# Starting a second wavefront earlier, and issuing a second layer in another order

## The chip, the cores and the metric

The kernel runs on one core of a Trainium2 chip. The time is that of the device for one execution, in microseconds (us). Before the change it is 12678.93 us, the median of three runs (12673.02 to 12680.4). A core has five engines, each with a queue of its own that it works off in order: TensorE (PE, with weight loads shown apart as PEld), VectorE (DVE), ScalarE (ACT), GpSimd (POOL), and SyncE (SP), which here only issues transfers (DMA). ACT issues some transfers too.

## The reference

The input is a batch of 16 images, 64 x 64 pixels, 128 channels, in float32. Two layers follow each other, each as x + layer(groupnorm(x)) with 32 groups of four channels.

The first layer is a two-dimensional recurrence. The cell at row i, column j needs h and c of the cell above and of the cell to the left:

```
f0 = sigmoid(pf0 + h_u @ uf0);  f1 = sigmoid(pf1 + h_l @ uf1);  hsum = h_u + h_l
it = sigmoid(pi + hsum @ ui);   ot = sigmoid(po + hsum @ uo);   cp = tanh(pc + hsum @ uc)
c  = f0*c_u + f1*c_l + it*cp;   h  = ot * tanh(c)
```

The p's are products of the normed pixel with weights of 128 x 128.

The second layer is a Mamba block (256 inner channels, 16 states, a causal convolution of four taps) over the 4096 pixels of each image, once forwards and once backwards; the results are added:

```
h = dA_t * h + dBx_t;   y_t = sum over states of h * C_t      (for each channel and state)
y = (y + xc * D) * silu(z);   out = y @ out_w.T
```

## The kernel before

**First layer** (`layer0`, L761 to L941). Cells on one anti-diagonal of an image do not need each other. So the work goes diagonal by diagonal: 127 diagonals (`ND`), of 1 to 64 and back to 1 cells. The 16 images are two groups of eight; a group is a *wavefront* (w = 0 or 1), and a diagonal of n cells is one tile of 128 channels x 8n columns.

- `statistics(b, q)` (L781) loads a quarter of image b on SP's queue (512 KB into `xs`, a ring of four buffers), transposes it on PE in eight blocks, and takes two DVE statistics. Four such *sets* make an image. The 32 sets of wavefront 0 run first; `normal(0)` (L805) makes scale and shift of the group norm from them. The 32 sets of wavefront 1 are `rest`.
- `load` (L841) reads the pixels of a diagonal, transposes and norms them (L855, L860). `cell` (L863) forms five gates: for each, a product with the pixel (L877) and one with the state (L878), accumulated in one PSUM bank, then an activation (L881). Then come the products with the old cell state on POOL (L889) and DVE (L890), input gate times candidate (L891), two additions (L892, L893), tanh on ACT (L894), and h on DVE (L895). `store` (L897) transposes h back, adds it to the pixels and writes `x1` from ACT's queue (L912).
- The list `steps` (L916 to L918) sets the order. Wavefront 1 begins `LATER` = 32 + 2 = 34 diagonals behind wavefront 0. So wavefront 0 is alone for 34 diagonals, then 93 pairs (one diagonal of each) follow, then wavefront 1 is alone for 34.
- A step does one piece of side work (L924 to L933): a set of statistics while `rest` has any; then `normal(1)`; then the zeroing of one of 12 matrices in memory; then a piece of `begin`, the start of the second layer: its weights, reading image 0 in eight parts, its group norm and its eight normalisations. The weights come from step 81 on, the rest from three steps after wavefront 0 has finished.

Within the first layer a scheduler at build time orders the instructions of each queue from this program.

**Second layer** (`layer1`, L944 on). An image is 16 *passes*: eight pieces of 512 pixels forwards (passes 0 to 7), and eight backwards (8 to 15). A pass has, for each of two halves of the 256 channels, 16 scans over 512 pixels on DVE (L1305), one for each state; ACT makes the decays (L1251); POOL makes 12 products of states with C (`out_of`, L1328), four drives (L1259) and two smaller products (`times`, L1232); PE makes the other drives (`drive_rows`, L1285), the convolution (`conv`, L1122), the sums over the states in transposed form (`sums`, L1365), and several transposes and projections. A backward pass has more for PE: the gate (L1141), adding the stored forward result (`again`), and the projection back (L1420, L1440). In forward passes the next image is read (L1038 to L1056); its group norm (`normal`, L1060 with L732 to L744) comes in pass 1, followed by eight normalisations on ACT (L1068). SP's queue issues all transfers of the layer, among them the states carried between passes (`keep`, L1317), the spread rows (L1204, L1210) and the scattered matrices (L1268, L1275).

The order of issue of all engines comes from `order_of_issue` (L300): it lists every operation of all 16 images with an engine, a cost (`COST`), what it must follow, and which ring of buffers it takes from (`RINGS`). `simulate` (L573) then runs through planned time; whenever an engine is free it takes, of the operations that are ready, the one with the least due time. The due time is 16 for each pass begun plus the operation's entry in the table `URGENCY` (L89). It has a number for every kind of operation in a pass, apart for forward and backward passes. The instructions are issued in exactly the order that comes out. So a change in the table moves operations within the queues, but neither adds nor drops any.

Of the kernel before, what the change touches and what calls it, by code (L numbers as in the profile page):

```python
# [8 lines left out]
F32 = mybir.dt.float32  # L9
# [5 lines left out]
P = 128  # L15
B, HH, WW, C = 16, 64, 64, 128
# [8 lines left out]
T = 512  # L25
# [19 lines left out]
def units_of(order):  # L45

    count = {}
    for x in order:
# [4 lines left out]
        else:  # L53
# [37 lines left out]
        {(0, 0): -19.08, (0, 1): 208.77, (0, 2): 213.67, (0, 3): 242.61, (1, 0): -194.98, (1, 1): -170.3,  # L91
         (1, 2): -208.38, (1, 3): -208.83},
        {(0, 0): 148.19, (0, 1): 250, (0, 2): 249.74, (0, 3): 231.08, (1, 0): -185.59, (1, 1): -186.03,
         (1, 2): -176.29, (1, 3): -177.49},
    ),
    "xproj": (
        {(): -6.34},
        {(): 83.3},
    ),
    "xproj_take": (  # L100
        {(): 46.52},
        {(): -25.9},
    ),
    "rows": (
        {(): 10.88},
        {(): -173.37},
    ),
    "bturn": (
        {(): 216.27},
        {(): -247.72},  # L110
    ),
    "bturn_take": (
        {(): -10.16},
        {(): 155.72},
    ),
    "dtproj": (
        {(0,): -166.35, (1,): -49.09},
        {(0,): -234.94, (1,): -199.34},
    ),
    "times": (  # L120
        {(0,): -141.19, (1,): -141.5},
        {(0,): -190.57, (1,): -223.42},
    ),
    "turn": (
        {(0,): 231.47, (1,): -199.74},
        {(0,): 155.15, (1,): 101.59},
    ),
    "turn_take": (
        {(0,): 35.4, (1,): 33.43},
        {(0,): 227.22, (1,): 227.05},  # L130
    ),
    "skip": (
        {(0,): -85.09, (1,): 194.24},
        {(0,): -59.43, (1,): 211.98},
    ),
    "spread": (
        {("b", 0): 55.31, ("d", 0): 221.01, ("c", 0): 249.78, ("c", 1): 249.59, ("d", 1): -104.59, ("c",
         2): 74.43, ("c", 3): 179.65, ("b", 1): 235.3, ("d", 2): 178.23, ("c", 4): 117.53, ("c", 5):
         216.75, ("k", 0): 205.82},
        {("b", 0): 49.04, ("d", 0): 82.05, ("c", 0): 58.5, ("c", 1): 225.69, ("d", 1): 85.64, ("c", 2):  # L140
         -52.53, ("c", 3): -84.56, ("b", 1): -71, ("d", 2): 188.69, ("c", 4): -46.09, ("c", 5): 139.95,
         ("k", 0): 79.7},
    ),
    "drive": (
        {(0, 0): -117.16, (1, 0): -45.65, (0, 1): -106.02, (1, 1): 204.54},
        {(0, 0): -55.01, (1, 0): -101.65, (0, 1): 78.56, (1, 1): 78.33},
    ),
    "decay": (
        {(0, 0): 214.71, (4, 0): 231.6, (5, 0): 235.97, (6, 0): 250, (7, 0): 244.04, (1, 0): -226.9, (8,
         0): 242.45, (9, 0): 229.56, (10, 0): 250, (11, 0): 196.68, (2, 0): 245.22, (12, 0): 142.99, (13,  # L150
         0): 196.62, (14, 0): 218.85, (15, 0): 250, (3, 0): 235.27, (4, 1): 237.55, (5, 1): 56.83, (6,
         1): 236.39, (7, 1): 200.04, (0, 1): 59.98, (8, 1): 241.45, (9, 1): 238.35, (10, 1): 238.37, (11,
         1): 237.94, (1, 1): 48.96, (12, 1): 223.29, (13, 1): 109.79, (14, 1): 109.58, (15, 1): 193.48,
         (2, 1): 244.06, (3, 1): 190.67},
        {(0, 0): 219.27, (4, 0): 159.93, (5, 0): 228.42, (6, 0): 227.96, (7, 0): 233.04, (1, 0): 162.12,
         (8, 0): 236.54, (9, 0): 145.98, (10, 0): -139.12, (11, 0): -88.73, (2, 0): -99.75, (12, 0):
         157.46, (13, 0): 250, (14, 0): 156.85, (15, 0): 167.22, (3, 0): 239.69, (4, 1): 187.28, (5, 1):
         236.16, (6, 1): 225.96, (7, 1): 248.99, (0, 1): 67.98, (8, 1): 248.77, (9, 1): 49.99, (10, 1):
         242.8, (11, 1): 168.72, (1, 1): 67.45, (12, 1): 163.7, (13, 1): 244.57, (14, 1): 244.31, (15,
         1): 176.22, (2, 1): 178.59, (3, 1): 181.09},  # L160
    ),
    "scan": (
        {(0, 0): -215.99, (4, 0): -197.78, (5, 0): -201.82, (6, 0): 171.7, (7, 0): -200.28, (1, 0):
         208.99, (8, 0): 81.27, (9, 0): 69.78, (10, 0): 50.84, (11, 0): 80.97, (2, 0): -179.33, (12, 0):
         -157.48, (13, 0): -159.07, (14, 0): -158.42, (15, 0): -158.71, (3, 0): -148.7, (4, 1): 17.61,
         (5, 1): 34.08, (6, 1): 7.6, (7, 1): 7.23, (0, 1): 145.62, (8, 1): 26.88, (9, 1): 56.47, (10, 1):
         26.63, (11, 1): 52.08, (1, 1): 203.51, (12, 1): 173.49, (13, 1): 174.73, (14, 1): 173.35, (15,
         1): 173.11, (2, 1): 173.02, (3, 1): -185.61},
        {(0, 0): 211.65, (4, 0): 208.82, (5, 0): 213.32, (6, 0): 210.34, (7, 0): 234.88, (1, 0): 234.81,
         (8, 0): 82.08, (9, 0): 81.92, (10, 0): 11.04, (11, 0): 61.9, (2, 0): 80.26, (12, 0): 96.06, (13,  # L170
         0): 93.07, (14, 0): 44.04, (15, 0): 82.19, (3, 0): 68.39, (4, 1): -115.05, (5, 1): -159.13, (6,
         1): -144.43, (7, 1): -169.42, (0, 1): -152.48, (8, 1): -158.76, (9, 1): -192.29, (10, 1):
         -192.53, (11, 1): -193.7, (1, 1): 178.94, (12, 1): 148.84, (13, 1): 136.94, (14, 1): 136.65,
         (15, 1): 184.35, (2, 1): 182.44, (3, 1): 227.69},
    ),
    "scatter": (
        {("d", 0): -98.3, ("d", 1): 226.02, ("d", 2): -35.02, ("k", 0): 142.02},
        {("d", 0): 197.57, ("d", 1): 181.75, ("d", 2): -137.41, ("k", 0): 53.02},
    ),
    "drive_rows": (  # L180
        {(0, 0): 86.02, (1, 0): -84.84, (2, 0): 123.21, (0, 1): 206.34, (1, 1): 117.75, (2, 1): 194.74},
        {(0, 0): 241.28, (1, 0): -59.19, (2, 0): -162.71, (0, 1): -157.55, (1, 1): -215.22, (2, 1):
         175.52},
    ),
    "keep": (
        {(0, 0): 250, (1, 0): -11.9, (2, 0): 227.54, (3, 0): -221.6, (4, 0): 195.72, (5, 0): -92.62, (0,
         1): 62.29, (1, 1): 169.33, (2, 1): 81.35, (3, 1): -229.04, (4, 1): 142.26, (5, 1): -18.73},
        {(0, 0): -186.63, (1, 0): 100.75, (2, 0): 123.12, (3, 0): -226.46, (4, 0): 126.26, (5, 0):
         182.78, (0, 1): -126.19, (1, 1): 179.51, (2, 1): -247.02, (3, 1): -146.55, (4, 1): -45.3, (5,
         1): 57.7},  # L190
    ),
    "out_of": (
        {(0, 0): 6.28, (1, 0): 110.81, (2, 0): 0.41, (3, 0): 46.99, (4, 0): 204.64, (5, 0): 230.6, (0,
         1): 26.46, (1, 1): 164.53, (2, 1): -138.94, (3, 1): -244.66, (4, 1): -239.51, (5, 1): -149.12},
        {(0, 0): -174.66, (1, 0): -174.81, (2, 0): 72.48, (3, 0): 7.85, (4, 0): 129.81, (5, 0): 102.68,
         (0, 1): -122.95, (1, 1): -122.04, (2, 1): -117.06, (3, 1): -192.11, (4, 1): -39.91, (5, 1): 57.1},
    ),
    "sums": (
        {(0, 0): 147.01, (1, 0): 204.95, (2, 0): 18.42, (3, 0): 110.12, (4, 0): -165.71, (5, 0): -154.21,
         (0, 1): 227.07, (1, 1): 180.09, (2, 1): 194.99, (3, 1): 242.48, (4, 1): 216.64, (5, 1): -169.16},  # L200
        {(0, 0): -212.32, (1, 0): -162.81, (2, 0): -161.63, (3, 0): -161.82, (4, 0): -157.85, (5, 0):
         -158.54, (0, 1): 73.85, (1, 1): 109.31, (2, 1): 81.83, (3, 1): 248.19, (4, 1): 249.43, (5, 1):
         249.81},
    ),
    "keep_group": (
        {(0, 0): -194.35, (0, 1): -163.44},
        {(0, 0): -239.33, (0, 1): -182.43},
    ),
    "turned": (
        {(0, 0, 0): -203.27, (0, 0, 1): 190.03, (0, 0, 2): 9.82, (0, 0, 3): -96.4, (0, 1, 0): 229.53, (0,  # L210
         1, 1): -154.5, (0, 1, 2): -157.58, (0, 1, 3): -113.93},
        {(0, 0, 0): -157.81, (0, 0, 1): 123.6, (0, 0, 2): -144.76, (0, 0, 3): -39.63, (0, 1, 0): 248.86,
         (0, 1, 1): 248.61, (0, 1, 2): 248.52, (0, 1, 3): 239.67},
    ),
    "turned_take": (
        {(0, 0, 0): 113.8, (0, 0, 1): 75.95, (0, 0, 2): 42.34, (0, 0, 3): 42.24, (0, 1, 0): 247.32, (0,
         1, 1): 153.61, (0, 1, 2): 153.43, (0, 1, 3): 222},
        {(0, 0, 0): 64.54, (0, 0, 1): 69.77, (0, 0, 2): 68.43, (0, 0, 3): 67.62, (0, 1, 0): -249.7, (0,
         1, 1): -214.46, (0, 1, 2): 155.94, (0, 1, 3): 155.85},
    ),  # L220
    "weigh": (
        {(0, 0): -250, (0, 1): -131.3},
        {(0, 0): -179.49, (0, 1): -150.84},
    ),
    "finish": (
        {(0,): 43.55, (1,): 250},
        {(0,): -158.64, (1,): 234.04},
    ),
    "spill": (
        {(): 111.19},  # L230
        {},
    ),
    "read_load": (
        {(): -159.46},
        {},
    ),
    "read_turn": (
        {(): 120.8},
        {},
    ),  # L240
    "read_take": (
        {(): 144.64},
        {},
    ),
    "read_stats": (
        {(): 1.05},
        {},
    ),
    "gate": (
        {},  # L250
        {(0,): -158.22, (1,): -164.04},
    ),
    "recall": (
        {},
        {(): -141.83},
    ),
    "again": (
# [1238 lines left out]
```

## Time and profile before

The profile is of one execution of its own, which took 12716.73 us.

| | |
|---|---|
| median of 3 runs | 12678.93 us |
| profiled execution | 12716.73 us, span 12714.9 us |
| granted TensorE clock, mean | 0.993 |
| PE busy / PE weight loads | 12144.3 us (96%) / 9452.5 us (74%) |
| DVE / ACT / POOL busy | 11120.1 (87%) / 9944.8 (78%) / 10600.8 us (83%) |
| first write of h / last write of h (end of first layer) | 89.1 / 1553.1 us |
| POOL products of states with C (L1328) | 3072, 2430 ns each |
| DVE scans with a drive from PE (L1305) | 5376, 1261 ns each, next one starting before the last ends |

How to read it: times are microseconds from the start of the span, and means of one instruction are in ns. An instruction's line is that of the kernel before. "out<-in" names the tile written and those read. A bracket `[1.2 <-PE py]` says that the engine was idle 1.2 us before the instruction, and which instruction ended that. PE overlaps its instructions and their ends are modelled; the distance from one start to the next is the safer measure. The granted clock is the share of full speed that PE was given.

### The profile page before, as it was taken

How to read it: one execution, taken by the hardware profiler on the slowest of the kernel's cores; microseconds unless marked ns; L12 is line 12 of the kernel's file. 1: busy time of each engine (PE TensorE's matmuls, PEld its weight loads, DVE VectorE, ACT ScalarE, POOL GpSimd, SP SyncE). 2: the span in 40 equal slices, each digit the busy share in tenths (PEclk: the TensorE clock that was granted, in tenths of full speed). 3: DMA queues.
4: the chain of work that ended last, by engine and by line, in shares of the span. 5: the costliest groups of instructions: out<-in, count | busy, mean ns of one | idle time of the engine just before them, and what ended most of it. 6: DMA issues, size and time to landing. Idle time of an engine off the chain costs nothing. (4 is left out here: it accounts for less than half of the span.)

```text
span 12714.9 us, 322475 instructions
## 1 busy us (share of the span) xinstructions
PE 12144.3 (96%) x128820; PEld 9452.5 (74%) x128820; DVE 11120.1 (87%) x11409; ACT 9944.8 (78%) x15935; POOL 10600.8 (83%) x4868
## 2 busy tenths in 40 slices
PE   8999999999999999999999999999999999999999
PEld 7666777777777777777777777777777777777777
DVE  6676599998989899999999998999989898989998
ACT  3444488888888888888888888888888888888887
POOL 0111199999999999999999998999999999999998
PEclk8999999999999999999999999999999999999999
DMA  4222155555555555555555555555555565556564
GB/s 151 54 57 55 49 157 162 159 159 158 164 160 156 160 161 158 159 165 156 164 159 160 158 164 158 163 161 156 160 159 160 156 163 156 158 158 164 155 163 138
DMA packets 2320784, 1885.93 MB, mean 148 GB/s; under 512 B 1537697, under 2 KB 1883313, under 8 KB 2319281
## 3 DMA queue, kind: packets, MB, share of 16 engines
q1 hardware_dynamic: 2241328, 1830.04, 52.2%
q10 hardware_dynamic: 77952, 35.24, 1.2%
q8 instruction: 1017, 16.66, 0.5%
q14 instruction: 487, 3.98, 0.1%
HBM read 1698.25 MB, written 164.30 MB: 146 GB/s over the span
## 5 line engine op out<-in xcount | busy, mean ns | idle before, releaser
L1328 POOL TENSOR_TENSOR hc<-hst,cr 128x1024 f32<-128x1024 f32 x3072 | 7380.5, 2430 | 416.6 <-DVE hst L1305 308.6
L1305 DVE TENSOR_TENSOR_SCAN hst<-da,carry,hps 128x512 f32<-128x512 f32 x5376 | 6452.1, 1261 | 497.7 <-issue 266.5
L1251 ACT ACTIVATE da<-dt,A_log_sb 128x512 f32<-128x512 f32 x8192 | 5386.9, 710 | 907.0 <-DVE hst L1305 814.8
L1365 PEld LDWEIGHTS py<-ident,hc 128*128 128x128 f32 x24576 | 2760.8, 141 | 685.1 <-issue 322.3
L1365 PE MATMUL py<-ident,hc 128*128 128x128 f32 x24576 | 3136.2, 275 | 139.2 <-POOL hc L1328 135.8
L1259 POOL TENSOR_TENSOR group<-dtx,br 128x1024 f32<-128x1024 f32 x1024 | 2448.6, 2405 | 150.2 <-PE ptg L1337 80.0
L1305 DVE TENSOR_TENSOR_SCAN group<-da,carry,group 128x512 f32<-128x512 f32 x1792 | 2236.1, 1267 | 203.7 <-ACT da L1251 199.5
L1285 PEld LDWEIGHTS hps<-d,dtxt 32*128 32x128 f32 x49152 | 1522.7, 186 | 731.7 <-issue 389.2
L1285 PE MATMUL hps<-d,dtxt 32*128 32x128 f32 x49152 | 1804.9, 283 | 211.1 <-DVE hst L1305 128.3
L1122 PE MATMUL pp<-xT,wk 128*128 128x512 f32 x4096 | 1994.7, 600 | 2.4 <-ACT dt L1226 1.2
L1345 ACT COPY ht<-ptg 128x512 f32<-128x512 f32 x2048 | 1130.4, 588 | 414.8 <-PE ptg L1337 390.3
L889 POOL TENSOR_TENSOR a_f<-a_f,c 128x288 f32<-128x288 f32 (+40 forms) x254 | 211.3, 832 | 1338.2 <-ACT a_f L881 1272.4
L1337 PE MATMUL ptg<-ident,group 128*128 128x128 f32 x8192 | 1154.3, 276 | 50.2 <-DVE group L1305 27.0
L1337 PEld LDWEIGHTS ptg<-ident,group 128*128 128x128 f32 x8192 | 926.5, 141 | 273.5 <-issue 106.2
L1122 PEld LDWEIGHTS pp<-xT,wk 128*128 128x128 f32 x4096 | 681.6, 191 | 420.6 <-issue 390.4
L1305 DVE TENSOR_TENSOR_SCAN hst<-da,hps 128x512 f32<-128x512 f32 x768 | 876.3, 1200 | 124.4 <-POOL hc L1328 38.2
L1232 POOL TENSOR_TENSOR dtx<-dt,xc 128x512 f32<-128x512 f32 x512 | 650.4, 1286 | 198.1 <-ACT dt L1226 168.2
L1251 ACT ACT_TABLE_LOAD x527 | 676.1, 1283 | 9.7
L1365 PE MATMUL py<-ddiag,xc 128*128 128x128 f32 x4096 | 579.3, 284 | 12.3 <-ACT y L1412 11.3
L1352 PE MATMUL py<-ht,k 128*32 128x128 f32 x16384 | 557.7, 276 | 0.8
L1365 PEld LDWEIGHTS py<-ddiag,xc 128*128 128x128 f32 x4096 | 496.8, 191 | 54.4 <-ACT y L1412 15.6
L1216 PE MATMUL pv<-dbl,dt_wT 128*128 128x256 f32 x2048 | 531.2, 392 | 0.2 <-DVE st L1056 0.2
(112 smaller groups left out, 12155.8 us busy)
## 6 DMA issues: line engine op xcount, KB each, us to landing
cr<-rows SPq DMA_DIRECT2D x1536, 512.0 KB
d<-d SPq DMA_DIRECT2D x768, 448.0 KB
br<-rows SPq DMA_DIRECT2D x512, 512.0 KB
k<-k SPq DMA_DIRECT2D x256, 256.0 KB
yf<-y SPq DMA_DIRECT2D x128, 512.0 KB
yl<-yf SPq DMA_DIRECT2D x128, 512.0 KB
carry<-hst SPq DMA_DIRECT2D x3072, 1.0 KB
xs<-in_x_dram SPq DMA_DIRECT2D x64, 512.0 KB
```

The costliest lines, as they stand in the source:

```text
L1122: nc.tensor.matmul(self.ps["conv", h], lhsT=wk[:, k, h * P : (h + 1) * P], rhs=xT[self.b % 2][:, t0 : t0 + T], start=(k == 0), stop=(k == ...
L1216: nc.tensor.matmul(pv[:, q * TQ : (q + 1) * TQ], lhsT=dt_wT[:, q, h * P : (h + 1) * P], rhs=self.dbl, start=True, stop=True,)
L1232: nc.gpsimd.tensor_mul(self.dtx[h], self.dt[h], self.xc[h])
L1251: nc.scalar.activation(t, self.dt[h], AF.Exp, scale=amat[:, h, s : s + 1])
L1259: nc.gpsimd.tensor_mul(both[:, m : m + 2, :], bc(self.dtx[h], 1, 2), self.brow[q])
L1285: nc.tensor.matmul(part[:, j, :, :], lhsT=self.dtxt[h][rows, j, :], rhs=dg[rows, j + r, :, :], start=True, stop=True, skip_group_check=True,)
L1305: nc.vector.tensor_tensor_scan(t[:, self.rev], self.da.pop((s, h))[:, self.rev], dbx[:, self.rev], 0.0 if self.first else carry[:, self.d, ...
L1328: nc.gpsimd.tensor_mul(self.hc[g, h], self.hst[g, h].rearrange("p t m -> p m t"), self.crow[g])
L1337: nc.tensor.transpose(pt[:, k, :], self.group[g, h][:, t0 : t0 + TB, :].rearrange("p t s -> p (t s)"), ident,)
L1345: nc.scalar.copy(t, self.ps.pop(("turned", g, h, j)))
L1352: nc.tensor.matmul(self.py[h][q * TB : (q + 1) * TB, j * P : (j + 1) * P], lhsT=cd[:, GX * j + q, :], rhs=self.ht[g, h, j][:, q, :], start ...
L1365: nc.tensor.matmul(self.py[h][:, cols], **{"start": False, "stop": False, **how}, skip_group_check=True)
```

## The change

It has two parts.

In the first layer, three sets of statistics are taken per step while `rest` has any, so `LATER` becomes 11 + 2 = 13; the ring of loads has eight buffers instead of four; the gates are formed in the order f0, f1, i, c, o, with the candidate before the output gate; and of `begin` up to two pieces are issued per step, each part of image 0 as soon as wavefront 0 has passed its rows by three steps.

In the second layer every entry of `URGENCY` but a few changes, and nothing else. The numbers come from a longer search over all images.

```diff
 URGENCY = {
     "conv": (
-        {(0, 0): -19.08, (0, 1): 208.77, (0, 2): 213.67, (0, 3): 242.61, (1, 0): -194.98, (1, 1): -170.3,
-         (1, 2): -208.38, (1, 3): -208.83},
...
+        {(0, 0): 226.07, (0, 1): 225.5, (0, 2): 209.71, (0, 3): 245.13, (1, 0): -224.93, (1, 1): -215.88,
+         (1, 2): -217.49, (1, 3): -219.71},
...
     "session": (
-        {(0,): 241.85, (1,): 239.93},
-        {(0,): 173.19, (1,): 69.9},
+        {(0,): 219.11, (1,): 226.41},
+        {(0,): 244.88, (1,): 9.25},
     ),
 }
...
-    gates = ["f0", "f1", "i", "o", "c"]
+    gates = ["f0", "f1", "i", "c", "o"]
...
-            xs = xp.tile([P, SB, C], F32, name=f"xs_{b}_{q}", tag="xs", bufs=4)
+            xs = xp.tile([P, SB, C], F32, name=f"xs_{b}_{q}", tag="xs", bufs=8)
...
-            f0, f1, it, ot, cand = act
+            f0, f1, it, cand, ot = act
...
-        LATER = len(rest) + 2
+        AT_ONCE = 3
+        LATER = -(-len(rest) // AT_ONCE) + 2
...
-        ready = steps.index((ND - 1, 0)) + 3
+        ready = [steps.index((WW - 1 + (c + 1) * T // WW - 1, 0)) + 3 for c in range(NCH)]
+        ready = [81] + ready + ready[-1:] * (len(begin) - NCH - 1)
...
             if rest:
-                statistics(*rest.pop(0))
+                for m in range(min(AT_ONCE, len(rest))):
+                    statistics(*rest.pop(0))
             elif 1 not in norm:
                 normal(1)
-                zeros = xp.tile([P, SB * C], F32, name="zeros", tag="xs", bufs=4)
+                zeros = xp.tile([P, SB * C], F32, name="zeros", tag="xs", bufs=8)
...
-            elif n > 80 and begin and (len(begin) == FIRST or n >= ready):
-                begin.pop(0)(lambda name: psum.tile([P, T], F32, name=name, tag="misc"))
+            else:
+                for m in range(2):
+                    if begin and n >= ready[FIRST - len(begin)]:
+                        begin.pop(0)(lambda name: psum.tile([P, T], F32, name=name, tag="misc"))
```

## The prediction

> **What bounds the kernel now.** I read the stages first (busy time of each engine in stretches of the span), because the page's shares are means over two very different layers; then the timeline inside each stage, for what is back to back and what waits; then the waits; the chain of waits last, and it is of little use here, since it covers only the last instructions. In the stage rows the columns are the stretch, its length, and then PE, PE weight loads, DVE, ACT and POOL busy, the granted TensorE clock, DMA share and GB/s. The first layer:
>
> ```profile
> 20.00:76.00 56.00, 38.27 (x224) 32.41 (x224) 40.41 (x71) 1.51 (x2) 0.00 (x0) 0.80 0.85 282
> 89.00:128.00 39.00, 39.00 (x184) 36.89 (x185) 17.81 (x70) 10.18 (x37) 1.56 (x6) 0.50 0.30 92
> 151.00:256.00 105.00, 102.46 (x651) 90.89 (x652) 85.90 (x252) 47.84 (x130) 12.46 (x21) 1.00 0.51 161
> 830.00:1397.00 567.00, 562.41 (x2367) 372.00 (x2366) 391.43 (x904) 249.07 (x553) 88.12 (x92) 0.99 0.20 53
> 1397.00:1500.00 103.00, 87.16 (x539) 77.77 (x537) 68.93 (x220) 57.05 (x146) 12.48 (x21) 1.00 0.15 39
> 1500.00:1553.00 53.00, 48.87 (x274) 46.61 (x274) 20.63 (x112) 21.07 (x78) 3.94 (x13) 0.66 0.05 12
> ```
>
> Up to 76 us the first half's statistics are read. From the 254 writes of h (L895, DVE) I date the diagonals: wavefront 0 alone from 89.2 to 256.4 us (34 diagonals), 93 pairs of diagonals from 256.4 to 1396.6, wavefront 1 alone to 1553.3. In the pairs PE is busy 562 of 567 us. That is real work: a 512-column product of two passes starts every 0.86 us in the timeline (1.67 ns per column), so a gate product on a diagonal of n cells (8n columns) takes 0.0133n us, with a floor of 0.21 us (0.43 measured at half clock near 114 us), and a 128-column transpose follows the next after 0.109 us. A diagonal costs ten products and a transpose in and out per 16 cells: for 46 and 48 cells 12.5 + 1.3 = 13.8 us, against 13.9 measured (832.4 to 846.3). Summed over the 93 pairs this is 1078.8 us of PE work in 1140.2 us: 0.66 us per pair is all that is not work. So pairing hides latency, but not work.
>
> The second layer, image 8: its passes 0 to 2, 3 to 7, and 8 to 15.
>
> ```profile
> 7137.90:7275.30 137.40, 124.56 (x1433) 97.60 (x1432) 119.74 (x111) 119.51 (x187) 122.18 (x55) 1.00 0.57 156
> 7275.30:7482.10 206.80, 194.56 (x2299) 152.58 (x2298) 193.76 (x164) 175.24 (x273) 203.57 (x92) 1.00 0.59 161
> 7482.10:7833.30 351.20, 348.80 (x3911) 274.89 (x3910) 318.11 (x279) 288.71 (x446) 326.20 (x145) 1.00 0.59 162
> ```
>
> Passes 3 to 7 have POOL as limit (203.6 of 206.8 us), passes 8 to 15 PE (348.8 of 351.2), and only passes 0 to 2 have no full engine. By the first scan of each pass, over images 1 to 14, the periods are 46.1, 51.2, 40.1 us for passes 0 to 2, 41.1 to 41.8 for 3 to 7, and 43.98 for each of 10 to 13, equal to 0.01 us in every image: a queue that is never empty. PE's timeline there shows each group starting where the last ends:
>
> ```profile
> 7526.15 1.04 PE L1365 MATMUL py<-ident,hc 128*128 128x128 f32 x8
> 7527.03 0.60 PE L1337 MATMUL ptg<-ident,group 128*128 128x128 f32 x4
> 7527.46 1.04 PE L1365 MATMUL py<-ident,hc 128*128 128x128 f32 x8
> 7528.34 1.02 PE L1122 MATMUL pp<-xT,wk 128*128 128x512 f32 x2
> ```
>
> The stalls of passes 1 and 2 are the group norm of the next image, on three engines in order:
>
> ```profile
> 7222.27 0.16 DVE L734 TENSOR_TENSOR dev_l<-mv,pm_l 128x1 f32<-128x1 f32 x1 [1.21 <-PE pm_l L732]
> 7224.27 0.16 DVE L742 RECIPROCAL scale_l<-std_l 128x1 f32<-128x1 f32 x1 [1.84 <-ACT std_l L740]
> ...
> 7228.34 4.79 POOL L1328 TENSOR_TENSOR hc<-hst,cr 128x1024 f32<-128x1024 f32 x2 [2.25 <-DVE hst L1305]
> 7237.86 2.38 POOL L1259 TENSOR_TENSOR group<-dtx,br 128x1024 f32<-128x1024 f32 x1 [4.74 <-PE ptg L1337]
> ```
>
> **The change part by part, first layer.** (1) *Shift 13 instead of 34.* The same 254 cells run; 21 diagonals of 14 to 34 cells at the head and 21 at the tail are no longer alone but make 21 more pairs. Alone they take 105.5 us (150.9 to 256.4) and 103.3 us (1396.6 to 1499.9). Their PE work by the prices above is 76.5 us each time; as pairs they cost 153.0 + 21 x 0.66 = 166.9 us. Gain 41.9 us. The largest pair now has some 115 cells, where DVE, at 391 of 567 us, still has room. (2) *Small pairs.* The first full and last three pairs of before were 0.8 to 1.6 us above the rest (10.0 us where the work is 7.8): +8 us for five or six such pairs of the new ends; 0 to +30. (3) *Three sets of statistics per step.* 32 sets now fall on the first 11 steps instead of 32. A set is eight PE transposes, two DVE statistics of 0.69 us and a 512 KB load on SP's queue. In the steps of diagonals 1 to 12 each DVE step becomes 6 x 0.69 + nine short operations of about 0.2 us = 6.0 us, behind which PE (24 x 0.109 + 2.3 = 4.9 us at full clock) and the load (1.5 MB at the 282 GB/s of the first row = 5.6 us) have room. Ten such steps, two lighter ones and the group norm of the second half with its two table loads make about 77 us; these steps take 61.7 us now, at half clock. +15 us. If the sets hid behind everything but PE it would be 12 x 4.9 = 59 us (-3); with PE at half clock for the whole head, a step takes 24 x 0.22 + 10 x 0.43 = 9.6 us, 11 of them and 4 us 110 us (+48).
>
> The clock is the doubt here: from 89 to 128 us it was granted at 0.50 although PE was busy without a gap, and full only when the diagonals reached 8 cells; the stretch 20 to 76 us, where PE did nothing but transposes, had 0.80. A head with three times the transposes resembles the second row more than the first, hence 77. [...]
>
> (4) *Eight buffers for the loads* instead of four: SP now issues eight sets ahead and no diagonal loads between. The first 20 us moved 182 GB/s, the next 56 us 282; at 282 from the start 20 x (1 - 182/282) = 7 us go. -7, between 0 and -18 (the whole 16.8 MB at the best 314 GB/s of 20 to 40 us, 54 us plus 4 us of landing, instead of 76). (5) *Candidate before output gate.* ACT does the output gate while DVE multiplies and adds, so the wait of ACT for the cell state shrinks by one activation (0.22 to 0.4 us). In pairs PE covers it, nothing gained; if that cover were gone ACT's waits for c (84 us in the whole profile) are the most it could bring. In 26 diagonals alone 0.3 us each: -8, between 0 and -40. (6) *Reading image 0 earlier.* Eight reads (four transposes, 0.69 us on DVE, 0.58 on ACT) move from the tail into pairs, where 0.44 us of PE each is 3.5 us; their loads wait on SP for the stores of diagonals three steps old, and the diagonal loads behind them are up to eight buffers ahead, so nothing is late; the group norm and eight normalisations of 0.80 us on ACT stay in a tail whose diagonals are shorter: +4 in sum, 0 to +10. The zeroing loads and SP's order cost nothing: DMA share is 0.20 in that stage. Sum: -41.9 + 8 + 15 - 7 - 8 + 4 = -30 us.
>
> **Second layer.** Every instruction and every table load stays (four per pass, 1.28 us); only places in queues differ. *Passes 8 to 15.* PE's order changes in some 30 places of a pass (sums, conv, both dtproj side by side before drive_rows, bturn three groups later); POOL swaps one drive with one out_of; the store's addition on DVE moves behind two scans, SP's scatter some five places. The sum of PE's pitches in the new order is the same to 0.05 us per pass. So at best nothing; a cover that breaks costs what PE then waits. 0; -6 to +51 (0.4 us in each of 128 passes, as long as DVE's waits for PE get in this stage). *Passes 3 to 7.* POOL and DVE keep their order word for word; POOL's 0.5 to 1.0 us of idle per pass is all there is: 0, +-16. *Passes 0 to 2.* 137.4 us against 3 x 40.5 us of POOL's pitches: 15.9 us per image, 254 us in all, is the end of the range below. But the norm keeps its place between the same scans, the 4.74 us wait keeps its cause (the last turned of pass 1, behind the same scans and normalisations), and drive_rows of pass 0 moves behind one sums and one read; I see some swaps that help and as many that don't. I take -1 us per image, -16; from -110 (half of the slack) to +40.
>
> [...]
>
> Sum of both layers: -46 us. The profiled execution took 12716.73 us (span 12714.9); the median of the runs is 12678.93, 0.3% less, and I take the difference off that: 12633 us. No change is within 0.2%, or 25 us.
>
> **Rivals.** *A, the slack of passes 0 to 2 is really won:* for it, 15.9 us per image without a full engine; against it, the norm in its old place. Half of it: -30 - 127 = 12522. *B, slower: PE's closed cycle breaks in the second passes.* The new order puts dtproj's pair and drive_rows before xproj, and bturn behind three turned; if one of them waits on ACT or DVE, everything behind it on PE waits, and nothing gives it back. It decides from 55/128 = 0.43 us per pass on; at 0.8 us (102 us) the time is 12678.93 - 30 + 102 = 12751. For it, eight passes per image with no spare PE time; against it, that POOL and DVE have 25 and 33 us per 351 to spare. *C, the head eats the gain:* half clock to the last set, +48 instead of +15, with little from the second layer: 12678.93 - 30 + 33 = 12682, no change. *D, the naive one:* the 42 single diagonals vanish behind others, -105 us: refuted by the pitches, unless PE's busy time is not work.
>
> **How the numbers follow.** Forecast 0.50, A 0.13, B 0.17, C 0.17, D 0.03. The forecast's own range is 12585 to 12655. The 8-in-10 range reaches into A and over C: 12545 to 12718. Faster: forecast, A and D but a little, 0.64; same: C and what is left, 0.19; slower 0.17.
>
> **What would show it.** Right: the first layer ends about 30 us earlier (h's last write near 1523); 114 pairs take 1300 to 1320 us; the second passes stay at 43.98. Wrong: a clock of 0.5 up to the last set of statistics; PE waits in passes 8 to 15; passes 0 to 2 well under or over 137 us.

## The result, and the profile after

The changed kernel takes **12571.66 us** (median; 12569.18 to 12577.5), the kernel before 12676.69 us in the same comparison. The ratio is 0.9917, with a 95% interval of 0.9904 to 0.9931: 105 us, or 0.8%, faster. The forecast was 12633 us. So the direction was right, and the time lies inside the range of 12545 to 12718, but below the forecast's own range (12585 to 12655): the gain is more than twice the 46 us that were worked out. That the wide range held is in part luck: its lower end was there for rival A, and what rival A describes did not happen (below).

The profiled execution has a span of 12567.3 us. The stages of the first layer, with the same columns as before (stretch, length, PE, PE weight loads, DVE, ACT, POOL busy, granted clock, DMA share, GB/s):

```profile
20.00:66.00 46.00, 37.58 (x224) 28.62 (x223) 38.33 (x70) 4.16 (x6) 0.00 (x0) 0.83 1.00 384
66.00:79.00 13.00, 12.49 (x64) 12.43 (x65) 7.21 (x21) 1.94 (x7) 0.21 (x1) 0.54 0.51 164
79.00:149.00 70.00, 63.60 (x489) 58.89 (x488) 54.01 (x176) 23.29 (x77) 3.89 (x12) 0.90 0.63 214
149.00:256.00 107.00, 106.56 (x770) 100.40 (x771) 76.14 (x313) 59.18 (x203) 16.71 (x34) 0.98 0.20 57
931.00:1443.00 512.00, 507.16 (x2466) 379.82 (x2464) 368.43 (x966) 247.53 (x594) 71.42 (x98) 1.00 0.20 52
1443.00:1506.00 63.00, 58.48 (x284) 55.66 (x284) 23.06 (x117) 30.43 (x91) 3.93 (x13) 0.56 0.06 14
```

The first half's statistics are read by 66 us, ten earlier than before, at 384 GB/s. From 79 to 149 us wavefront 0 runs its first diagonals beside three sets of statistics per step, at a mean clock of 0.90. Then come pairs, with PE full, until 1443. The last 13 diagonals of wavefront 1 run alone, at a mean clock of 0.56. The last write of h is at 1506.3 us, against 1553.3.

The second layer, image 8: passes 0 to 2, 3 to 7, 8 to 15, and of the last group pass 8 alone and passes 10 to 13.

```profile
7053.00:7187.60 134.60, 124.92 (x1432) 99.38 (x1431) 119.70 (x111) 119.46 (x187) 120.79 (x55) 0.99 0.58 157
7187.60:7392.40 204.80, 192.55 (x2280) 150.42 (x2279) 191.11 (x161) 173.72 (x270) 201.96 (x90) 1.00 0.59 161
7392.40:7741.10 348.70, 346.81 (x3913) 275.89 (x3912) 319.42 (x280) 287.56 (x444) 326.66 (x146) 1.00 0.58 163
7392.40:7434.90 42.50, 40.84 (x470) 32.09 (x469) 37.26 (x35) 33.55 (x53) 42.50 (x20) 1.00 0.63 175
...
7478.60:7653.40 174.80, 174.65 (x1969) 139.50 (x1968) 161.40 (x142) 145.41 (x226) 162.81 (x73) 1.00 0.58 161
```

POOL is still the limit of passes 3 to 7 and PE that of passes 9 to 15, now at 43.7 us per pass where it was 44.0. In pass 8 it is POOL, without a gap. The group norm's place in pass 1 has not changed, as the timelines of POOL and DVE show:

```profile
7134.57 0.16 DVE L732 TENSOR_TENSOR dev_l<-mv,pm_l 128x1 f32<-128x1 f32 x1 [0.47 <-PE pm_l L730]
7136.57 0.16 DVE L740 RECIPROCAL scale_l<-std_l 128x1 f32<-128x1 f32 x1 [1.84 <-ACT std_l L738]
```

```profile
7151.48 2.39 POOL L1262 TENSOR_TENSOR group<-dtx,br 128x1024 f32<-128x1024 f32 x1 [5.25 <-PE ptg L1340]
```

The wait of 1.84 us for ACT is the same, and POOL's long wait for the turned group (a `group` tile that PE has transposed, `ptg`) is 5.25 us, not shorter than the 4.74 us of before.

One caution on all comparisons of single profiles. The profiled execution of before was 40 us over its median. By the first scans of the passes its mean image took 695.6 us; the first run below has the same order of the second layer and took 692.5. Where this document costs the second layer it compares with that run.

### The profile page after: what moved, and what is told of

Its sections match the earlier page's. It is cut to its first block, busy times and chain, and to the rows that moved or that the text cites. A ratio compares the mean times of both kernels' runs of the same rounds, so it can differ in the third digit from the quotient of the medians.

```text
span 12567.3 us, 322625 instructions
## 1 busy us (share of the span) xinstructions
PE 12114.5 (96%) x128820; PEld 9486.8 (75%) x128820; DVE 11138.3 (89%) x11409; ACT 9954.8 (79%) x15936; POOL 10578.2 (84%) x4868
## 5 line engine op out<-in xcount | busy, mean ns | idle before, releaser
L1125 PE MATMUL pp<-xT,wk 128*128 128x512 f32 x4096 | 1954.8, 599 | 1.7 <-ACT dt L1229 1.2
L887 POOL TENSOR_TENSOR a_f<-a_f,c 128x16 f32<-128x16 f32 (+35 forms) x254 | 188.6, 743 | 1313.9 <-ACT a_f L879 1250.2
L879 ACT ACTIVATE a_f<-pg_f,b_sb 128x16 f32<-128x16 f32 (+35 forms) x508 | 219.7, 472 | 415.2 <-DMA x<-xl 212.7
```

What stands on the lines that cost most here:

```text
L879: nc.scalar.activation(agv.rearrange("p i b -> p (i b)"), pgv, AF.Tanh if g == "c" else AF.Sigmoid, bias=b_sb[:, gi : gi + 1],)
L1125: nc.tensor.matmul(self.ps["conv", h], lhsT=wk[:, k, h * P : (h + 1) * P], rhs=xT[self.b % 2][:, t0 : t0 + T], start=(k == 0), stop=(k == ...
```

## The experiments

### The two parts, each alone

The first layer's change with the old table:

```diff
 (changed kernel)
-URGENCY = { new entries }
+URGENCY = { entries of the kernel before }
```

> The whole change of the first layer, with the old table of due times in the second. In the profiles the last write of h of the changed kernel comes 47 us earlier (1506.3 against 1553.3 us). If that gain reaches the end undiminished, the time is the median of before less 47: 12630 us, within 5. The second layer's profile tells a second thing: the profiled execution of before was 40 us over its median. If that was chance, the mean image of the second layer, 695.3 us there, is about 692.5 us here; if the old order really costs 695 us, it is 695 again. The rival that the first layer's gain is given back later (the second layer waits for something else) would leave 12660 or more.

Measured: 12643.88 us (12625.6 to 12663.8) against 12680.88, ratio 0.9971 (0.9962 to 0.998): 37 us, and 14 us more than the 12630 us expected. The mean image took 692.5 us, as foreseen; the last write of h came at 1532.5 us, not 1506.

The new table with the old first layer:

```diff
 (kernel before)
-URGENCY = { old entries }
+URGENCY = { entries of the changed kernel }
```

> The kernel before with the new table of due times alone. If the two parts add, this is 12571.7 + 47 = 12619 us, 58 us under before, or 3.6 us per image. If the whole difference of the two profiled second layers (100 us) is real, it is 12577 us. My prediction had 16 us here, 12661 us; its rival A (half of the slack of passes 0 to 2) 127 us, 12550 us. Rival A needs the gain in passes 0 to 2; the theory that the profiles suggest has it spread over all passes, by about 0.35 us each.

Measured: 12594.86 us, ratio 0.9938 (0.9924 to 0.9951): 86 us, 24 us under the sum of the two parts that was expected (12619). So the table is the larger part, and it is worth some five times the 16 us that I gave it. Alone, the parts give 37 and 86 us; together 105, and 111 in a later comparison (below). Such sums are good to some 15 us, since single runs of one kernel spread by 20 to 40 us, and I don't read a loss into the difference.

What the second layer gained, and where, is read from the distances of the first scans of each pass, as means over images 1 to 14. The second row is the mean over seven profiles with the new order (the changed kernel twice, and five of the others here):

| us per image | passes 0-2 | 3-7 | 8 | 9 | 10-13 | 14-15 | all |
|---|---|---|---|---|---|---|---|
| old order (first run) | 136.3 | 205.1 | 43.1 | 44.1 | 176.0 | 87.8 | 692.5 |
| new order | 135.7 | 205.2 | 41.9 | 43.8 | 174.9 | 87.7 | 689.1 |

The row of pass 8 in the old order, in image 8, shows no engine full (PE 40.94, POOL 40.83 of 43.00 us):

```profile
7449.50:7492.50 43.00, 40.94 (x474) 32.02 (x472) 36.99 (x34) 33.57 (x53) 40.83 (x19) 1.00 0.64 191
```

Of 3.4 us per image (54 us in all), 2.7 are in passes 8 to 15, which I had put down as without any possible gain, and only 0.7 in passes 0 to 2, where I looked for it.

### What PE saves in a second pass

In passes 10 to 13 PE has no gap in either order, and the same instructions take 44.01 and 43.73 us. I added up the distances from each PE start to the next by kind, in the two kernels above. Some names from the kernel's list of operations are needed: `dtproj` is the projection that gives the step sizes (`pv` in the lines below), `xproj` the one before it (`pd`), `bturn`, `turn` and `turned` are transposes on PE (`pbt`, `ptx`, `ptg`), and `weigh` is a product with 32 columns of weights (`py<-ht,k`). Of the 0.28 us, 0.21 belong to dtproj's eight products (2.03 to 1.82 us), 0.08 to conv (7.16 to 7.08) and 0.07 to the sums; drive rows and turn give 0.07 back. The timeline of before shows dtproj's two halves apart, behind xproj and behind bturn:

```profile
7549.00 1.08 PE L1159 MATMUL pd<-xc,x_wT_sb 128*64 128x256 f32 x8
7550.02 1.13 PE L1216 MATMUL pv<-dbl,dt_wT 128*128 128x256 f32 x4
7551.08 1.17 PE L1285 MATMUL hps<-d,dtxt 32*128 32x128 f32 x32
7552.18 1.17 PE L1179 MATMUL pbt<-ident,dbl 64*64 64x64 f32 x16
7553.28 1.13 PE L1216 MATMUL pv<-dbl,dt_wT 128*128 128x256 f32 x4
7554.25 1.60 PE L1337 MATMUL ptg<-ident,group 128*128 128x128 f32 x12
```

and that of the changed kernel shows them side by side, behind a sum:

```profile
7415.46 1.92 PE L1368 MATMUL py<-ident,hc 128*128 128x128 f32 x16
7417.22 1.89 PE L1219 MATMUL pv<-dbl,dt_wT 128*128 128x256 f32 x8
7419.05 1.17 PE L1288 MATMUL hps<-d,dtxt 32*128 32x128 f32 x32
```

Start to start, before: 1.06 + 0.97 = 2.03 us; after: 1.83. No wait stands in these lines. The groups beside dtproj have small tiles (32x128, 128x64, 64x64 weights), and in both traces a change to such a tile costs: the last product of conv is followed after 0.43 us by a sum or a turned, but after 0.52 us by drive rows or weigh: 0.09 us on the way in. There is a price on the way out too, 0.10 us: from start to start, the first of dtproj's products takes 0.32 us behind xproj or bturn and 0.22 behind a sum, and the first of conv's 0.53 behind drive rows and 0.43 elsewhere; the products in the middle of dtproj take 0.22 us in both orders, and those in the middle of conv 0.43.

The two prices together give the gain. If each PE product of the new order gets the price that its kind has in the profile of before, by whether the next one has a small tile, the estimate for a pass is 43.96 us, as good as the 43.98 of before. If the price also goes by whether the product in front has a small tile, the estimate is 43.72 us; the profiles of the new order have 43.71 to 43.76.

To try it I swapped two neighbours on PE, so that groups with small tiles stand together:

```diff
+def side_by_side(order, eng):
+    on_pe = [o for o in order if eng[o[:3]] == "PE"]
+    for a, b in zip(on_pe, on_pe[1:]):
+        swap = (a[0], a[2], b[0], b[2])
+        if swap == ("turn", (1,), "drive_rows", (2, 1)) or swap == ("bturn", (), "turn", (0,)):
+            order.remove(a)
+            order.insert(order.index(b) + 1, a)
+    return order
```

> The changed kernel with two swaps of neighbours in PE's queue, in nearly every pass: the last turn behind the drive rows after it, and bturn behind the first turn. Both put products with small tiles (32, 64 or 128x32 weights) next to each other. Theory: what shortened the second passes by 0.28 us is PE's own pitch, which depends on what follows; in both traces a full product followed by one with a small tile costs 0.09 us more (conv 0.52 instead of 0.43, dtproj 0.31 instead of 0.22). Two such changes less should bring passes 10 to 13 from 43.74 to 43.56 to 43.65 us, 12 to 23 us in all. Rival: the pitch is not the cause, the period stays 43.74. Second rival: any order but the searched one breaks, by microseconds per pass, as the two half tables did.

Measured: 12617.54 us, and passes 10 to 13 at 44.12 us instead of 43.73. The period rose by 0.4. The second rival seems to have it, but PE's timeline shows both effects apart:

```profile
7502.48 1.53 PE L1350 MATMUL ptg<-ident,group 128*128 128x128 f32 x12
7504.40 0.72 PE L1252 MATMUL ptx<-ident,dtx 128*128 128x128 f32 x4 [0.38 <-ACT ht L1358]
7505.05 1.17 PE L1192 MATMUL pbt<-ident,dbl 64*64 64x64 f32 x16
```

The turn (ptx) now waits for ACT's copy of the turned group, which frees its bank. Bturn, 1.1 us of PE work, had covered that wait. From the last turned to the turn it is 0.65 us in the mean, 0.11 between two products of one turned: 0.54 us of wait. The pitch of turn itself fell by 0.12 us, from 1.36 to 1.24. So the cheaper neighbours were real, and the cover that the swap took away cost more. The other swap alone went into the last kernels below.

### Half of the new table

```diff
 (changed kernel; each entry of URGENCY is a pair: forward passes, backward passes)
-    kind: (new, new),
+    kind: (new, old),    # the other run: (old, new)
```

> The changed kernel, with the new due times in forward passes only and the old ones in backward passes. If the halves are independent, the gain of the profiles divides as the passes show it (2.7 us per image in passes 0 to 7, 3.0 in passes 8 to 15), and with 58 us in all this is 12571.7 + 31 = 12603 us. If the backward passes can gain nothing, as the prediction had it, it is near 12572. If the two halves only fit each other (rival), the border passes 0 and 8 get longer and the time is 12630 or more, above the first layer's change alone.

> The opposite half: new due times in backward passes, old ones in forward passes. Halves independent: 12571.7 + 27 = 12599 us, and passes 10 to 13 at the changed kernel's 43.74 us. Backward passes without gain: 12630 us. Halves that only fit each other: above 12630 us, with the loss in passes 0 and 8.

Measured: 13220.57 and 13968.53 us, 4% and 10% slower than before. Both of my main theories are wrong by far, and the rival had too small a price and, for the first run, the wrong place (passes 0 and 8). With new forward entries alone it is the backward passes that suffer, at 47.6 to 52.4 us for passes 9 to 15. In passes 10 and following of image 8 the trace has 16 transposes of the next image's pixels, in four passes:

```profile
L1012 PE MATMUL pt<-ident,xl x16: 272/273/273, 7852.3 to 7995.1; 128*128 128x128 f32 x16
```

In the changed kernel that line has no instruction in passes 9 to 13. So the next image's reading, which belongs to forward passes, is issued in backward ones, and PE waits there for DVE's y. The waits are 7.3 us of the 20 us that these four passes take more, and cost more than themselves: the clock's mean is 0.97 in these passes, because three of the four longest are each followed by 3.4 us at 0.50. In image 15, which has no next one, backward passes take 44.0 us again. The two halves of the table are one scale of due times, on which work of the one competes with work of the other. The opposite half costs 66 us per image in forward passes and 20 in backward ones; what stands in the way there was not followed.

### The first layer: distance, and the small parts

Each small part alone would be lost in the spread, so one run has the small parts without the shift, the other the shift without the small parts, both with the new table.

```diff
 (changed kernel)
-        AT_ONCE = 3
+        AT_ONCE = 1
```

> The changed kernel with one set of statistics per step, so that the second wavefront is 34 diagonals behind again; eight buffers, the gates' new order, the earlier reads and the new table stay. If the small parts are worth what the prediction gave them (-7 for the buffers, -8 for the gates, +4 for the reads), the last write of h comes near 1534 us (1544.8 with none of them and the same table) and the time is some 12584 us. If they carry most of the first layer's gain (rival), the last write is near 1515 and the time that of the changed kernel, 12572.

```diff
 (kernel before, new table)
-        LATER = len(rest) + 2
+        AT_ONCE = 3
+        LATER = -(-len(rest) // AT_ONCE) + 2
...
-                statistics(*rest.pop(0))
+                for m in range(min(AT_ONCE, len(rest))):
+                    statistics(*rest.pop(0))
```

> The complement: the kernel before with the new table, three sets per step and the second wavefront 13 diagonals behind; four buffers, the old order of the gates and the old reads. By the prediction's first three terms (-42 + 8 + 15) this is 19 us under the new table alone: 12576 us, and the last write of h near 1526. The pairs between the twelfth diagonal of wavefront 0 and the last 13 of wavefront 1 should take about 1300 us as in the changed kernel. If four buffers starve three sets a step (rival), the 32 sets take well over the 70 us that they take in the changed kernel.

Measured: 12581.83 us for the small parts (expected 12584) and 12578.1 for the shift (expected 12576); the new table alone had 12594.86. The times fit, though 13 and 17 us are no more than single runs of one kernel spread. The last writes of h do not fit: they were expected near 1534 and 1526 us and came at 1520.6 and 1511.3. The stages, from the writes of h, say more. The third column runs from wavefront 0's diagonal 12 to wavefront 1's diagonal 113, the fourth over the last 13 diagonals:

| us | first h | head, to diagonal 12 | middle | tail | last h |
|---|---|---|---|---|---|
| before | 89.2 | 61.7 | 1349.0 | 53.4 | 1553.3 |
| new table only | 84.9 | 61.4 | 1346.7 | 51.8 | 1544.8 |
| small parts, no shift | 76.6 | 60.1 | 1332.3 | 51.6 | 1520.6 |
| shift, no small parts | 86.7 | 73.8 | 1288.2 | 62.6 | 1511.3 |
| changed kernel | 78.9 | 70.0 | 1294.1 | 63.3 | 1506.3 |
| changed kernel, later run | 77.3 | 66.2 | 1302.4 | 63.3 | 1509.2 |

- The shift takes 58 us off the middle, and gives 12 back in the head and 11 in the tail. The reading of image 0 falls into the tail in this run, but does not explain the 11 us: the changed kernel reads earlier, and its tail takes 63.3 us. What goes with the length is the clock: 0.66 in the tail of before, 0.62 in this one, 0.56 in that of the changed kernel.
- The eight buffers bring the first write forward, from 85 to 89 us to 76 to 79.
- With the old distance the small parts together take 14 us off the middle; which of them does was not separated. With the new distance they add 6 to 14 us: from step 80 to 126 (by wavefront 1's diagonals 67 and 113), into which the early reads fall, it takes 463 us (466 in the later run) instead of 455, and the tail gets no shorter for it.

### The clock of head and tail

The first layer's code of the changed kernel was profiled six times, in kernels that differ in the second layer only. Its last write of h came at 1506, 1509, 1509, 1519, 1533 and 1533 us. Most of the difference arises in the head, which took from 66 to 89 us. In the first run of this document (old table):

```profile
80.00:100.00 20.00, 20.00 (x96) 19.20 (x96) 11.20 (x36) 3.32 (x13) 0.49 (x2) 0.50 0.49 161
100.00:120.00 20.00, 19.97 (x94) 18.72 (x92) 10.99 (x31) 3.70 (x13) 0.56 (x2) 0.50 0.47 163
```

and in the later run of the changed kernel:

```profile
80.00:100.00 20.00, 18.72 (x158) 16.84 (x157) 16.77 (x54) 4.63 (x19) 0.76 (x3) 1.00 0.70 231
100.00:120.00 20.00, 19.13 (x167) 17.73 (x166) 18.57 (x58) 5.70 (x23) 1.24 (x4) 1.00 0.77 258
```

The program is the same, the clock 0.50 or 1.00, and with it 96 or 158 products in 20 us. PE is called busy in both. To see what holds the clock I gave PE more transposes:

```diff
+            if n < LATER or n >= len(steps) - LATER - 1:
+                warm = psum.tile([P, T], F32, name=f"warm_{n}", tag="misc")
+                for j in range(12):
+                    nc.tensor.transpose(warm[:, j % 4 * P : (j % 4 + 1) * P], ident, ident)
             after = load(*steps[n + 1]) if n + 1 < len(steps) else None
```

> The changed kernel with 12 more transposes of the unit matrix on PE, which nothing reads, in each of the first 13 and the last 14 steps of the first layer. Theory: the granted clock follows how much PE does, transposes included (in the changed kernel's head it was 0.9 to 1.0 with 24 transposes per step, and in the tail, with hardly any, 0.50). Then the tail's clock is 1.0 instead of 0.50 to 0.56, its 13 steps take 3.9 instead of 4.7 us, the head no longer has stretches at 0.5, and the time is 10 to 25 us less: 12547 to 12562. Rival: transposes do not count, the clock stays at 0.5, each takes 0.22 us in front of the products, and 27 steps of up to 2.6 us make the kernel slower, up to 12640.

Measured: 12569.47 us (12559.14 to 12585.54). The clock is what the theory said. The stretches are two of the head and one of the tail:

```profile
80.00:100.00 20.00, 20.00 (x177) 18.86 (x177) 15.69 (x48) 4.38 (x18) 0.76 (x3) 1.00 0.63 202
100.00:120.00 20.00, 20.00 (x180) 19.06 (x180) 16.49 (x50) 4.98 (x20) 0.91 (x3) 1.00 0.78 259
...
1480.00:1500.00 20.00, 20.00 (x173) 18.93 (x171) 7.95 (x46) 8.37 (x30) 1.26 (x5) 1.00 0.03 7
```

The tail took 55.4 us instead of 63.3, and the head 73.9, in the middle of its six values without the transposes. In the median little of it is left: 12569 is above the expected 12547 to 12562, and 2 us under the changed kernel in its first comparison, less than single runs spread. Transposes do hold the clock here: the tail has 0.56 without them and 0.99 with them.

The opposite came from a still smaller distance:

```diff
-        AT_ONCE = 3
+        AT_ONCE = 8
```

> The changed kernel with eight sets per step, so that the second wavefront is 6 diagonals behind. DVE limits the head: 32 sets of 2 x 0.69 us with the short operations of four steps are about 55 us, so the head ends some 8 us earlier; seven diagonals become pairs at 5.3 us (37 us), and seven steps of the tail at 4.7 us (33 us) go, with seven of the head that are in the 8 us already. Together -3 us: 12565 to 12600, no difference. Rival: fewer single diagonals always pay, as from 34 to 13 (33 us); then another 10 us or more.

Measured: 12617.76 us, 45 us slower than the changed kernel beside it (12573.06). Neither theory had that. After the statistics, pairs of a few cells follow each other, and the clock falls:

```profile
140.00:160.00 20.00, 20.00 (x96) 19.34 (x95) 5.78 (x36) 6.69 (x26) 1.14 (x4) 0.50 0.16 57
160.00:200.00 40.00, 40.00 (x185) 38.25 (x185) 13.70 (x74) 14.05 (x50) 2.90 (x8) 0.50 0.07 17
```

A pair takes 9.5 us there, where I had counted 5.3; the next pair once the clock is full, at 207 us, takes 5.0. The groups of PE in 160 to 200 us show why PE can be full and the clock low: wavefront 0 has 9 to 13 cells there and wavefront 1 three to seven, so the products have 24 to 104 columns. Each product is two passes, and each pass is one instruction in these lines: 0.42 us long in the mean, but overlapping its neighbours. From start to start a pass takes 0.21 us whatever its columns (0.11 in the tail above, at 1.00; in the profile of before, passes of 8 to 64 columns start 0.213 us apart at 0.50 and 0.112 at 1.00).

```profile
L875 PE MATMUL pg_f<-xn,w_sb 128*128 128x80 f32 (+8 forms) x36 | 10.6, 420 | 0.0
L876 PE MATMUL pg_f<-h,u_sb 128*128 128x80 f32 (+7 forms) x32 | 9.6, 421 | 0.0
L875 PE MATMUL pg_o<-xn,w_sb 128*128 128x24 f32 (+8 forms) x18 | 5.6, 413 | 0.0
```

The other end pays the same. The last 13 diagonals of wavefront 1, seven of them now in pairs, take 104.8 us instead of 63.3:

```profile
1500.00:1540.00 40.00, 40.00 (x185) 37.74 (x184) 11.86 (x72) 13.70 (x51) 2.17 (x8) 0.50 0.06 16
```

PE was busy for 40.00 of 40 us here, at 0.50. Products of few columns, one behind the other (24 to 104 columns from 160 to 200 us), did not bring the full clock; with transposes of 128 columns between small products, in the tail above, it was 1.00 from 1480 to 1500 us.

The profiles say more. The clock changes only in steps of 3.41 us (in the profile of before its stretches last 3.41, 6.83, 10.24, 17.07, 51.20 us and other multiples). I counted the columns that PE's instructions of the first layer stream in each such window (each pass of a product by itself), from 5 to 1490 us in all 14 profiles: 5575 windows have 1800 columns or more, and the next window has the full clock every time, though 64 of them ran at 0.50 themselves; 299 have under 1400, and the next has 0.50 every time, though 67 of them ran at 1.00; the 195 between go either way. So the clock follows the columns streamed in a window here, transposes included, and not PE's busy time. This also explains how one program can have both clocks: in the first of the two heads above, a window at 0.50 passes 984 to 1616 columns, until one with 1816 is followed by the full clock, near 127 us; in the second, at 1.00, the same work passes 1768 to 3264, and the clock stays at 1.00. The second layer, where many products have small tiles, does not follow this count: in the profiles of before and after, 13 windows of 2054 to 4614 columns are followed by 0.50. No run changed the columns alone.

### What the runs point to, in one kernel

```diff
 (changed kernel, with the 12 transposes)
-        ready = [steps.index((WW - 1 + (c + 1) * T // WW - 1, 0)) + 3 for c in range(NCH)]
-        ready = [81] + ready + ready[-1:] * (len(begin) - NCH - 1)
+        ready = steps.index((ND - 1, 0)) + 3
...
+        if (a[0], a[2], b[0], b[2]) == ("turn", (1,), "drive_rows", (2, 1)):
+            order.remove(a)
+            order.insert(order.index(b) + 1, a)
```

> What the runs so far point to, in one kernel: the changed kernel with the 12 idle transposes in the first 13 and last 14 steps, with the old time of the reads of image 0 (each piece alone, from three steps after wavefront 0 has finished), and with one of the two swaps on PE, the last turn behind the drive rows. Each part shows in its own stretch of the profile. Reads: steps 80 to 126 took 454 us with the old reads and 463 with the early ones, so 454 here, 9 us less. Transposes: tail about 55 us at a clock of 1.0, head of about 71 us. Swap: bturn keeps its place as cover of the wait for turn, and turn's pitch alone falls by 0.12 us, so passes 10 to 13 take 43.6 us; if they take 43.74 or more, the swap is worth nothing. In all 12540 to 12560 us, below the changed kernel beside it.

> The changed kernel itself, on the same chip as the other three. Its first layer's code has been profiled five times, in the changed kernel and in four kernels that differ in the second layer only, and ended at 1506, 1509, 1519, 1533 and 1533 us, the later the longer the clock stayed at 0.50 after 80 us. If that is chance from run to run, the last write lies again between 1506 and 1533 and the single runs spread by some 20 us around 12580.

Measured: 12537.02 us (12525.11 to 12557.02), ratio to before 0.9885 (0.987 to 0.9901), beside the changed kernel with 12573.06 (12555.64 to 12579.92), 0.9912 (0.9898 to 0.9925). It is 36 us faster by the medians, 3 us under the range expected; by the profiles 22. Steps 80 to 126 took 457 us (466 beside it), the tail 58.0 (63.3), and passes 10 to 13 43.56 us (43.72): each of the three parts is there. Only the head is longer than beside it, 73.8 us where about 71 were expected (66.2). For the swap it is 0.16 us per pass; from start to start 0.09 of it is turn's, which no longer stands ahead of drive rows, and 0.10 that of the products with `ddiag`, which no longer stand behind them. The first layer ended at 1494.5 us. The changed kernel's own first layer ended at 1509 us, within what was expected.

> The first of these four with eight sets per step. By the same sum 3 us under it, no difference that can be measured; if head and tail are worth more than the sum says, 10 us or more under it.

Measured: 12586.05 us, slower again by 49. (Passes 10 to 13, with the swap here too, took 43.54 us.) The 12 transposes covered its first 6 and last 7 steps only, and from 160 to 200 us, behind them, the clock was 0.50:

```profile
160.00:200.00 40.00, 40.00 (x186) 38.42 (x186) 14.49 (x80) 14.02 (x51) 3.14 (x9) 0.50 0.06 17
```

Whether eight sets with transposes through all small pairs would pay was not tried.

## Why the prediction was right, and where not

The step that failed is the sentence on passes 8 to 15: "The sum of PE's pitches in the new order is the same to 0.05 us per pass. So at best nothing". The sum fell by 0.28 us in each of passes 10 to 13, because dtproj's halves, side by side, cost 0.21 us less than apart and conv has two small-tile followers less. I had priced each group by what follows it and not by what stands in front of it, though the trace of before shows both: behind xproj and bturn the first of dtproj's products takes 0.32 us instead of 0.22, and that price went with its neighbours. And pass 8 is not a pass with PE as its limit: it took 43.1 us with 40.9 of PE and 40.8 of POOL in the old order, so it had slack, and the new order took 1.2 us of it.

Term by term:

- *Shift with small pairs (-34).* The run with the shift alone took 58 us off the middle and put 11 on the tail: -47. The mechanism is as described; by the prediction's prices the 114 pairs have 1231.8 us of PE work, and they took 1288.2, 0.49 us more per pair and not 0.66, so the +8 us for small pairs were not needed.
- *Three sets (+15, from -3 to +48).* Six heads took 66 to 89 us, 76 in the mean, against 61.7: +14. But it is not one value: it is the clock's, 0.50 or 1.00 from run to run. Rival C, the head at half clock, happened in two of six profiles, at +27 us instead of +48, since the clock was full from some 127 us on.
- *Eight buffers (-7).* The first write came 10 us earlier (86.9 against 77 us in the mean).
- *Order of the gates (-8) and early reads (+4).* With the new distance they are +6 to +14 together, of which the reads, priced at 3.5 us there, are 8 to 12 by steps 80 to 126. That pairs are full of PE work, and that a read put into them costs its time, was in the prediction; that the tail would gain nothing by it was not.
- *First layer in all (-30).* The mean of the six executions ends at 1518 us, against 1549 for the two of the old distance: -31. The two medians say -37.
- *Passes 0 to 2 (-16).* -0.7 us per image, -11. The norm and the long wait kept their place and size, as argued; rival A is refuted as a mechanism, though the time came closer to its number.
- *Passes 3 to 7 (0).* 205.1 and 205.2 us.
- *Passes 8 to 15 (0, from -6 to +51).* -2.7 us per image, -44. The lower end was wrong.
- *Rival B.* No new wait of PE; passes 9 to 15 are full in both. But the swap of bturn showed the mechanism: there a lost cover of 0.54 us cost 0.4 us per pass.

The second layer was to give 16 us, and its own run gave 86 by the medians. By the passes it is 54 against one profile of the old order and 103 against the other (695.6 us per image). An estimate from the medians, less the mean end of the first layer in the profiles (1549 and 1518 us), lies between: 70 to 85 us. How much the old order varies from run to run was not settled.

## What to carry to other kernels

An engine without gaps can still get faster by order alone (44.01 to 43.73 us per pass here): add up real distances from start to start, with their means, by what stands in front of and behind each group. Before two neighbours are swapped, look for the wait that the first one covers (0.54 us here). An order found by a search may hold only as a whole: each half of these numbers gave a kernel slower than the one before, by 4 and 10%.

A busy PE at half clock looks like a full one (40.00 of 40 us at 0.50 here); read the granted clock beside it, stage by stage, and profile a stage more than once before a figure for it is trusted (the head took 66 to 89 us).

## What was not expected of the hardware

- A full PE (40.00 of 40 us) at a clock of 0.50, with products of 24 to 104 columns, a pass every 0.21 us; with 12 transposes of 128 columns per step the same kind of step has 1.00. In the first layer the next 3.41 us had the full clock whenever PE streamed 1800 columns or more in the last, and half of it below 1400.
- The same instructions of the head at 0.50 or at 1.00 from one execution to the next, 66 to 89 us.
- 0.09 us more behind a full product when the next has a small tile, and 0.10 us more for the first of dtproj's and of conv's products behind one.
